# One-hot graph attention with residual and layer norm: rows led by their own column taken from SBUF instead of being gathered

## The chip, the cores and the metric

One NeuronCore of a Trainium2 chip. The metric is the device time of the kernel in microseconds (us). Before the change three runs gave 233.75 to 234.14 us, median 233.87 us.

## The reference

Four attention heads over 4096 nodes with 512 features, then a residual and a layer norm:

```python
ht = (h @ W).reshape(N, H, D).transpose(1, 0, 2)            # per head
e = leaky_relu(src[:, :, None] + dst[:, None, :], 0.01) + adj_mat[None]
att = softmax(e, axis=-1)
h_prime = einsum('hij,hjd->hid', att, ht).mean(axis=0)
x = layernorm(x + h_prime)                                   # no scale, no bias, eps 1e-5
```

`x` is 4096x512 and `adj` 4096x4096, both float32 (8.4 MB and 67.1 MB). The entries of `adj` that are not zero are uniform up to 1e9, and the diagonal is always among them, while the scores that are added are small. So the softmax of a row is one-hot at the largest entry of its `adj` row, unless two entries lie very close, and then `h_prime[i] = x[j] @ mean_over_heads(W)` with j the column of the largest entry of row i. Low columns are more likely to be filled than high ones.

## The kernel before, in words

The 4096 rows are worked on in 32 blocks of 128 rows (128 partitions). Block 0 holds rows 0 to 127; row p of block ib >= 1 is row 128 + 31p + ib - 1. A branch to a general path is taken when some row has no clear leader; with these inputs it is not taken.

Each block goes through a pipeline, and the outer loop `for t in range(NB)` writes its stages out by hand; every engine runs its instructions in the order in which this loop issues them.

- SyncE issues all large loads on one queue: W and `adj` (2.1 MB for a block; six buffers `adj_t`, so five blocks ahead, `load_adj(t + AHEAD)`), and the residual's rows of `x` into `hold[:, ib, :]`, four blocks (1.05 MB) at a time, at the steps that `x_at` lists. The stores of the results come at the end on the same queue.
- VectorE at step t takes the maxima of segments of block t (`seg`, L212: segments of 16 columns in blocks 0 to 17, then 32, then 64), the largest segment (`top`, `at`, L222 and L224), and, for block t - 2, the place of the maximum inside the segment (`within`, L270).
- GpSimd turns these into row numbers and gathers: `lead` (the leading segment, L230) for block t, then `col` (the leading column, L272) and the rows of `x` that the columns name, `y` (L255), for block t - 2. Columns below 128 in blocks 1 to 27 (`TABLED`) are not gathered: `col` gets 8192 (`SKIP`) added, which is out of bounds, so the gather leaves that row of `y` as `clear_rows` (L245, ScalarE) left it: zero. Those rows come from a table of 128 ready products (`z`, split in three bf16 parts) by a one-hot matrix `pick` (`spread`, `from_table`).
- TensorE does block t - 3: the one-hot's broadcast `px` (L331), the transpose of `y` in four pieces (`tp`, L284), the residual (`ident` times `hold`, L296), the table (L343) and four products with the mean of W (L303). ScalarE copies `tp` to `yt` (L286) between the transposes and the products.
- ScalarE does the squares and sums for the layer norm and for the test for a clear leader, and at t + 1 clears the next `y`.
- `head_norms` (L469), three parts, makes the norms of W and a that the test needs.

In this text block b of `y` is gathered in step b + 2 of the loop and turned by TensorE in step b + 3; ScalarE's `clear_rows` for block b stands in step b - 1, ahead of the copy `yt` of block b - 4.

Of the kernel before, what the change touches and what calls it, by code (L numbers as in the profile page):

```python
# [21 lines left out]
P = 128  # L22
# [5 lines left out]
LAST = 4  # L28
SKIP = 8192
TABLED = range(1, 28)  # L30


@with_exitstack
# [40 lines left out]
def leading_rows(ctx, tc, x, adj, W, a, out, ident, leads, any_bad):  # L74
# [74 lines left out]
    load_x(0, 1)  # L149
    for ib in range(KB // 2 + 1, AHEAD):  # L150
        load_adj(ib)
    load_x(1, Q - 1)

    make_identity(nc, ident)
    first = once.tile([P, NB], U32, name="first")
    for e, lo, hi in spans:
        if lo == 0:
            nc.gpsimd.iota(first[:, 0:1], pattern=[[0, 1]], base=0, channel_multiplier=N // e)
            lo = 1
        nc.gpsimd.iota(  # L160
            first[:, lo:hi], pattern=[[N // e, hi - lo]], base=(P + lo - 1) * N // e,
            channel_multiplier=RB * N // e,
        )
    ones = once.tile([P, P], F32, name="ones")
    nc.gpsimd.memset(ones, 1.0)
    width = once.tile([P, len(spans)], U32, name="width")
# [6 lines left out]
    zero = once.tile([P, 1], F32, name="zero")  # L173
# [25 lines left out]
    low_of, pick_of = {}, {}  # L199

    def segment_maxima(ib, lo, hi):

# [14 lines left out]
    def find_segment(ib):  # L217
        if ib == NB - 1:
            nc.vector.max(out=top[:, ib, :], in_=best)
            return  # L220
        seg = seg_of.pop(ib)
        nc.vector.max(out=top[:, ib, :], in_=seg)  # L222
        at = at_of[ib] = small.tile([P, 8], U32, name="at")
        nc.vector.max_index(at, top[:, ib, :], seg)  # L224
        row = small.tile([P, 1], U32, name="row")
        nc.gpsimd.tensor_tensor(row, at[:, 0:1], first[:, ib : ib + 1], op=OP.add)  # L226
        k = span_of(ib)
        e = spans[k][0]
# [6 lines left out]
        start = at_of[ib] = small.tile([P, 1], U32, name="start")  # L235
        if ib in TABLED:
            away = small.tile([P, 1], F32, name="away")
            nc.gpsimd.tensor_scalar(away, at[:, 0:1], float(P // e), float(SKIP), op0=OP.is_lt, op1=OP.mult)
            nc.gpsimd.tensor_scalar(start, at[:, 0:1], float(e), away, op0=OP.mult, op1=OP.add)
        else:  # L240
            nc.gpsimd.tensor_tensor(start, at[:, 0:1], width[:, k : k + 1], op=OP.mult)

    def clear_rows(ib):
        y = y_t[ib] = y_pool.tile([P, D], F32, name="y")
        nc.scalar.copy(y, zero.to_broadcast([P, D]))  # L245

    def gather_rows(ib, col):
        if ib not in TABLED:
            y = y_t[ib] = y_pool.tile([P, D], F32, name="y")
            nc.gpsimd.indirect_dma_start(  # L250
                out=y, out_offset=None, in_=x,
                in_offset=bass.IndirectOffsetOnAxis(ap=col[:, :1], axis=0),
            )
            return
        nc.gpsimd.indirect_dma_start(  # L255
            out=y_t[ib], out_offset=None, in_=x,
            in_offset=bass.IndirectOffsetOnAxis(ap=col[:, :1], axis=0),
            bounds_check=N - 1, oob_is_err=False,
        )
        low = low_of[ib] = small.tile([P, 1], BF16, name="low")  # L260
        nc.gpsimd.tensor_scalar(low, col, float(SKIP - 1), float(SKIP - 1), op0=OP.max, op1=OP.subtract)

# [3 lines left out]
    def find_column(ib):  # L266
        if ib < BEHIND:
            find_inner(ib)
        within = small.tile([P, 8], U32, name="within")
        nc.vector.max_index(within, top[:, ib, :], lead_of[ib])  # L270
        col = small.tile([P, 1], U32, name="col")
        nc.gpsimd.tensor_tensor(col, at_of.pop(ib), within[:, 0:1], op=OP.add)  # L272
        gather_rows(ib, col)

    def find_column_in_row(ib):
# [2 lines left out]
        nc.vector.max_index(col, top[:, ib, :], adj_t[ib])  # L278
        gather_rows(ib, col)

    def turned_rows(y):
        tp = psum.tile([P, KB, P], F32, name="tp", bufs=2)
        for kb in range(KB):
            nc.tensor.transpose(tp[:, kb, :], y[:, ds(kb, P, KB)], ident)  # L284
        yt = rows.tile([P, KB, P], F32, name="yt")
        nc.scalar.copy(yt, tp)  # L286
        return yt

    def turn(ib):
        yt_of[ib] = turned_rows(y_t.pop(ib))  # L290

    def residual(ib):
        start = ib not in o_ps
# [35 lines left out]
    def spread(ib):  # L329
        where = psum.tile([P, P], F32, name="px", bufs=1)  # L330
        nc.tensor.matmul(where, low_of.pop(ib).to_broadcast([P, P]), ident_b, start=True, stop=True)  # L331
        off = rows.tile([P, P], F32, name="off")
        nc.scalar.activation(off, where, AF.Square, bias=minus)  # L333
        pick = pick_of[ib] = rows.tile([P, P], BF16, name="pick")
        nc.scalar.activation(pick, off, AF.Relu, bias=1.0, scale=-1.0)  # L335
# [193 lines left out]
    def report(pg):  # L529
        nc.vector.tensor_scalar(any_bad, pg, -1.0, float(N), op0=OP.mult, op1=OP.add)  # L530

    x_at = {lo - 1 - lo // (5 * Q): (lo, Q) for lo in range(Q, BEHIND, Q)}
    squares = list(range(KB * H))
    squares_at = {t: 2 if t < 7 else 1 for t in range(3, 15)}
    COLUMN, PROJECT, STATS = 2, 3, 4
# [10 lines left out]
    for t in range(NB):  # L546
# [325 lines left out]
```

## Time and profile before

| | |
|---|---|
| median of 3 runs | 233.87 us (233.75 to 234.14) |
| time of the profiled execution | 233.53 us |
| its span, first to last instruction | 232.0 us |
| mean granted TensorE clock | 0.98 |
| TensorE busy | 197.6 us (85%) |
| VectorE busy | 189.6 us (82%) |
| ScalarE busy | 153.2 us (66%) |
| GpSimd busy | 111.5 us (48%) |
| moved by DMA | 96.04 MB, mean 414 GB/s |

The span is the time from the first to the last instruction; 1.5 us of the execution lie outside it. The busy shares are averages over stages in which different engines wait. PE is TensorE, PEld its weight loads, DVE VectorE, ACT ScalarE, POOL GpSimd, SP SyncE. `L303` is line 303 of the kernel before.

### The profile page before, as it was taken

What the parts mean: (1) busy time and instruction counts of PE and PEld (TensorE: products, weight loads), DVE (VectorE), ACT (ScalarE), POOL (GpSimd) and SP (SyncE); (2) the same over time, 40 slices, a digit from 0 to 9 for tenths busy, and PEclk for the clock granted to TensorE, in tenths of its full rate; (3) what the DMA queues carried; (4) which work ended last, traced back from release to release, by engine and by line L of the source; (5) the groups of instructions that cost most, each with busy time, mean ns of one, the idle gap of its engine ahead of it and who ended that gap; (6) DMA issues with size and microseconds to landing.
All of it is one profiled execution on the core that took longest, in us unless ns stands there. A gap on an engine that the chain in (4) does not pass through costs nothing.

```text
span 232.0 us, 2532 instructions
## 1 busy us (share of the span) xinstructions
PE 197.6 (85%) x604; PEld 95.5 (41%) x614; DVE 189.6 (82%) x296; ACT 153.2 (66%) x378; POOL 111.5 (48%) x254
## 2 busy tenths in 40 slices
PE   0069988779099999997999899999999999999990
PEld 0033443334044444443444345454544444545460
DVE  0448289899879997999699959996999999967882
ACT  3003213588075987797998678878888877958872
POOL 4020414525554556355635665554565665637620
PEclk9999999999859999999999999999999999999997
DMA  6999999999999999999999999999999999999995
GB/s 221 426 435 428 433 421 437 425 431 411 440 429 422 420 437 427 429 421 434 418 433 430 417 435 429 419 430 431 426 432 415 419 425 416 419 416 419 420 374 207
DMA packets 13379, 96.04 MB, mean 414 GB/s; under 512 B 2148, under 2 KB 2596, under 8 KB 7984
## 3 DMA queue, kind: packets, MB, share of 16 engines
q1 hardware_dynamic: 9792, 88.08, 90.0%
q0 software_dynamic: 3552, 7.73, 8.5%
q8 instruction: 6, 0.10, 0.2%
q14 instruction: 13, 0.11, 0.1%
q10 hardware_dynamic: 16, 0.02, 0.0%
HBM read 88.51 MB, written 8.39 MB: 418 GB/s over the span
## 4 chain that ended last, share of the span: by engine, by line
DMA 44%; PE 30%; DVE 19%; ACT 2%; issue 1%; POOL 1%; DVEq 0%; POOLq 0%; ACTq 0%
DMA adj_t<-in_adj_dram 39%; PE o L303 19%; DVE seg L212 15%; DMA y<-in_x_dram,col 4%; PE o L296 3%; PE o L343 3%; PE tp L284 3%; PE o L400 2%; DVE at L224 1%; DVE top L222 1%; DMA a_rows<-in_L_gnn_a_dram 1%; DVE inner L264 1%; POOL lead L230 0%; PE o L396 0%; ACT sq L368 0%
## 5 line engine op out<-in xcount | busy, mean ns | idle before, releaser
L212 DVE TENSOR_REDUCE seg<-adj_t 128x128 f32<-128x2048 f32 (+4 forms) x54 | 138.9, 2589 | 27.4 <-DMA adj_t<-in_adj_dram 27.4
L303 PE MATMUL o<-w_sum,yt 128*128 128x512 f32 x248 | 113.5, 598 | 1.1 <-ACT yt L286 0.8
L303 PEld LDWEIGHTS o<-w_sum,yt 128*128 128x128 f32 x248 | 46.8, 192 | 49.0 <-issue 42.0
L230 POOL DMA_INDIRECT lead<-in_adj_dram,row x31 | 32.5, 1050 | 14.5 <-POOL row L226 14.5
L255 POOL DMA_INDIRECT y<-in_x_dram,col x27 | 29.1, 1077 | 12.1 <-POOL col L272 6.1
L226 POOL TENSOR_TENSOR row<-at,first 128x1 uint32<-128x1 uint32 x31 | 5.8, 188 | 60.0 <-DVE at L224 43.6
L284 PE MATMUL tp<-ident,y 128*128 128x128 f32 x128 | 22.9, 302 | 12.0 <-DMA y<-in_x_dram,col 11.9
L286 ACT COPY yt<-tp 128x512 f32<-128x512 f32 x33 | 19.0, 576 | 14.2 <-PE tp L284 13.9
L451 PE MATMUL o<-hold,ident 128*128 128x512 f32 x32 | 16.4, 671 | 14.0 <-DMA hold<-in_L_gnn_W_dram 14.0
L284 PEld LDWEIGHTS tp<-ident,y 128*128 128x128 f32 x128 | 18.3, 210 | 23.9 <-issue 17.8
L296 PE MATMUL o<-hold,ident 128*128 128x512 f32 x50 | 26.5, 612 | 0.0
L333 ACT ACTIVATE off<-px,minus 128x128 f32<-128x128 f32 x27 | 9.9, 366 | 19.9 <-PE px L331 19.8
L343 PE MATMUL o<-z,pick 128*128 128x512 bf16 x72 | 20.4, 386 | 1.1 <-ACT pick L335 0.8
L347 ACT ACTIVATE sq<-hold 128x512 f32<-128x512 f32 x32 | 20.0, 625 | 0.0
L391 ACT ACTIVATE hold<-hold,nm,sd 128x512 f32<-128x512 f32 x24 | 18.8, 801 | 0.0
L374 ACT ACTIVATE sq<-hold,nm 128x512 f32<-128x512 f32 x24 | 17.3, 722 | 0.8
L452 ACT ACTIVATE w_sum<-o 128x512 f32<-128x512 f32 x4 | 2.4, 597 | 22.5 <-PE o L451 22.5
L245 ACT COPY y<-zero 128x512 f32<-128x512 f32 x27 | 16.3, 603 | 0.0
L451 PEld LDWEIGHTS o<-hold,ident 128*128 128x128 f32 x32 | 6.7, 216 | 22.9 <-issue 21.6
L343 PEld LDWEIGHTS <-pick 128*128 128x128 bf16 x81 | 7.8, 100 | 19.9 <-issue 10.5
L372 ACT ACTIVATE hold<-o 128x512 f32<-128x512 f32 x24 | 14.3, 597 | 0.8
L222 DVE MAX8 top<-seg 128x8 f32<-128x256 f32 (+2 forms) x31 | 11.3, 366 | 1.1
(117 smaller groups left out, 190.3 us busy)
## 6 DMA issues: line engine op xcount, KB each, us to landing
adj_t<-in_adj_dram SPq DMA_DIRECT2D x28, 2048.0 KB, 33.1
adj_t<-in_adj_dram SPq DMA_DIRECT2D x6, 1024.0 KB, 27.3
out_dram<-hold SPq DMA_DIRECT2D x12, 512.0 KB, 10.1
hold<-in_x_dram SPq DMA_DIRECT2D x5, 1024.0 KB, 33.0
hold<-in_L_gnn_W_dram SPq DMA_DIRECT2D x2, 2048.0 KB, 16.5
hold<-in_x_dram SPq DMA_DIRECT2D x4, 512.0 KB, 12.7
adj_t<-in_adj_dram SPq DMA_DIRECT2D x4, 512.0 KB, 18.6
out_dram<-hold SPq DMA_DIRECT2D x4, 256.0 KB, 2.8
```

Source lines behind the costliest of these rows:

```text
L212: nc.vector.tensor_reduce(seg_of[ib][:, ts(k, N // e // n)], adj_t[ib][:, ts(k, N // n)].rearrange("p (s e) -> p s e", e=e), axis=AX.X, op ...
L230: nc.gpsimd.indirect_dma_start(out=lead, out_offset=None, in_=adj_segs[e], in_offset=bass.IndirectOffsetOnAxis(ap=row[:, :1], axis=0),)
L255: nc.gpsimd.indirect_dma_start(out=y_t[ib], out_offset=None, in_=x, in_offset=bass.IndirectOffsetOnAxis(ap=col[:, :1], axis=0), bounds_che ...
L284: nc.tensor.transpose(tp[:, kb, :], y[:, ds(kb, P, KB)], ident)
L286: nc.scalar.copy(yt, tp)
L296: nc.tensor.matmul(o_ps[ib], ident, hold[:, ib, :], start=start, stop=False)
L303: nc.tensor.matmul(o_ps[ib], yt_of[ib][:, kb, :], w_sum[:, kb, :], start=(start and kb == 0), stop=(kb == KB - 1),)
L343: nc.tensor.matmul(o_ps[ib], pick, z[k], start=(start and k == 0), stop=False)
L347: nc.scalar.activation(sq, hold[:, ib, :], AF.Square, accum_out=xx[:, ib : ib + 1])
L374: nc.scalar.activation(sq, hold[:, ib, :], AF.Square, bias=nm[:, i], scale=-float(D), accum_out=sd[:, i])
L391: nc.scalar.activation(hold[:, ib, :], o, AF.Identity, bias=nm[:, i], scale=sd[:, i])
L451: nc.tensor.matmul(o, ident, hold[:, w_at + kb * H + h, :], start=(h == 0), stop=(h == H - 1))
```

## The change

In blocks 4 to 17 (`OWNED`) a row whose leading column is its own row number is no longer gathered. `clear_rows` copies the block's rows of `x` from `hold` into `y` instead of zeros. GpSimd compares the column with the row's own number (`own`, made once), adds 8192 to it where they are equal (`skipped`, `asked`), and gathers with `asked`. What `y` then holds in the rows of the table is the row's own `x`, which must not count; so a masked identity `kept` (`ident * 8192 > col`) takes the place of `ident` when `y` is turned, and since that is no plain transpose any more, `nc.tensor.matmul` takes the place of `nc.tensor.transpose`. Columns are float32 in these blocks.

As `hold` must now be filled a step before the block's `y` is cleared, `x` is loaded sooner: blocks 1 to 7 in one load ahead of `adj` block 5, 8 to 11 at step 2, 12 to 15 at step 6, 16 to 19 at step 10 (before: 1 to 3 ahead, 4 to 7 at step 3, 8 to 11 at 7, 12 to 15 at 11, 16 to 19 at 15); 20 to 23 stay at step 18. The three parts of `head_norms` move from steps 21 to 23 to steps 16 to 18. The tile `off` becomes bf16 with one buffer. Near the end two normalising copies move ahead of a square root.

```diff
+OWNED = range(4, 18)
...
-    load_x(1, Q - 1)
+    load_x(1, 2 * Q - 1)
...
+    own = once.tile([P, len(OWNED)], F32, name="own")
+    nc.gpsimd.iota(
+        own, pattern=[[1, len(OWNED)]], base=P + OWNED[0] - 1, channel_multiplier=RB,
...
     def clear_rows(ib):
         y = y_t[ib] = y_pool.tile([P, D], F32, name="y")
-        nc.scalar.copy(y, zero.to_broadcast([P, D]))
+        nc.scalar.copy(y, hold[:, ib, :] if ib in OWNED else zero.to_broadcast([P, D]))
+
+    def leave_out_own(ib, col):
+        skipped = small.tile([P, 1], F32, name="skipped", bufs=2)
+        k = ib - OWNED[0]
+        nc.gpsimd.tensor_scalar(skipped, col, own[:, k : k + 1], float(SKIP), op0=OP.is_equal, op1=OP.mult)
+        asked = small.tile([P, 1], U32, name="asked", bufs=2)
+        nc.gpsimd.tensor_scalar(asked, col, skipped, None, op0=OP.add)
+        return asked
+
+    def keep_gathered(ib, col):
+        kept = kept_of[ib] = rows.tile([P, P], F32, name="kept")
+        nc.gpsimd.tensor_scalar(kept, ident, float(SKIP), col, op0=OP.mult, op1=OP.is_gt)
...
+        asked = leave_out_own(ib, col) if ib in OWNED else col
         nc.gpsimd.indirect_dma_start(
             out=y_t[ib], out_offset=None, in_=x,
-            in_offset=bass.IndirectOffsetOnAxis(ap=col[:, :1], axis=0),
+            in_offset=bass.IndirectOffsetOnAxis(ap=asked[:, :1], axis=0),
             bounds_check=N - 1, oob_is_err=False,
         )
+        if ib in OWNED:
+            keep_gathered(ib, col)
...
-    def turned_rows(y):
+    def turned_rows(y, kept=None):
...
-            nc.tensor.transpose(tp[:, kb, :], y[:, ds(kb, P, KB)], ident)
+            if kept is None:
+                nc.tensor.transpose(tp[:, kb, :], y[:, ds(kb, P, KB)], ident)
+            else:
+                nc.tensor.matmul(tp[:, kb, :], y[:, ds(kb, P, KB)], kept, start=True, stop=True)
...
-        off = rows.tile([P, P], F32, name="off")
+        off = rows.tile([P, P], BF16, name="off", bufs=1)
...
-    x_at = {lo - 1 - lo // (5 * Q): (lo, Q) for lo in range(Q, BEHIND, Q)}
+    x_at = {2: (8, 4), 6: (12, 4), 10: (16, 4), 18: (20, 4)}
...
-        if 21 <= t < 24:
-            head_norms(t - 21)
+        if 16 <= t < 19:
+            head_norms(t - 16)
...
     add_sums(NB - 2, hold[:, NB - 2, :])
+    finish(BEHIND + 2)
+    finish(LATE - 1)
     moments(NB - 2)
-    finish(BEHIND + 2)
     stats_of_half(NB - 1, 0)
     factor(NB - 2)
     normalise(NB - 2, o_ps.pop(NB - 2))
-    finish(LATE - 1)
```

SyncE's queue, from the load of x's first rows on. Before (`x4` at a row's end counts equal rows; a row of x with 128x1536 is three blocks, with 128x2048 four):

```order
L132 DMA hold<-in_x_dram 128x512
L128 DMA adj_t<-in_adj_dram 128x4096 x2
L135 DMA hold<-in_x_dram 128x1536
L128 DMA adj_t<-in_adj_dram 128x4096 x3
L135 DMA hold<-in_x_dram 128x2048
L128 DMA adj_t<-in_adj_dram 128x4096 x4
L135 DMA hold<-in_x_dram 128x2048
```

After:

```order
L133 DMA hold<-in_x_dram 128x512
L129 DMA adj_t<-in_adj_dram 128x4096 x2
L136 DMA hold<-in_x_dram 128x3584
L129 DMA adj_t<-in_adj_dram 128x4096 x2
L136 DMA hold<-in_x_dram 128x2048
L129 DMA adj_t<-in_adj_dram 128x4096 x4
L136 DMA hold<-in_x_dram 128x2048
```

The load of seven blocks of x stands where that of three stood, ahead of `adj` block 5, and the next two loads of x stand ahead of `adj` blocks 7 and 11 instead of 8 and 12; the one after that, ahead of 15 instead of 16.

GpSimd for one block (the gather of block 4 in step 6; `lead` there is block 6's). Before:

```order
L226 TENSOR_TENSOR row<-at,first 128x1
L230 DMA lead_442<-in_adj_dram,row 128x16
L238 TENSOR_SCALAR away<-at 128x1
L239 TENSOR_SCALAR start<-at,away 128x1
L272 TENSOR_TENSOR col<-start,within 128x1
L255 DMA y<-in_x_dram,col 128x512
L261 TENSOR_SCALAR low<-col 128x1
```

After:

```order
L232 TENSOR_TENSOR row<-at,first 128x1
L236 DMA lead_445<-in_adj_dram,row 128x16
L245 TENSOR_SCALAR away<-at 128x1
L246 TENSOR_SCALAR start_f<-at,away 128x1
L297 TENSOR_SCALAR col_f<-within,start_f 128x1
L258 TENSOR_SCALAR skipped<-col_f,own 128x1
L260 TENSOR_SCALAR asked<-col_f,skipped 128x1
L276 DMA y<-in_x_dram,asked 128x512
L265 TENSOR_SCALAR kept<-ident,col_f 128x128
L284 TENSOR_SCALAR low<-col_f 128x1
```

Two small operations stand between `col` and the gather, and `kept` (128x128) between the gather and `low`.

TensorE around the first part of `head_norms`. Before it stands between blocks 17 and 18:

```order
L303 MATMUL o<-w_sum,yt 128x512 x4
L475 MATMUL o<-ww,ones 128x16
L476 MATMUL o<-each,ones 128x8
L331 LDWEIGHTS low
L331 MATMUL px<-ident_b,low 128x128
L284 MATMUL tp<-ident,y 128x128 x4
L296 MATMUL o<-hold,ident 128x512
```

After, between blocks 12 and 13:

```order
L334 MATMUL o<-w_sum,yt 128x512 x4
L506 MATMUL o<-ww,ones 128x16
L507 MATMUL o<-each,ones 128x8
L362 LDWEIGHTS low
L362 MATMUL px<-ident_b,low 128x128
L315 MATMUL tp<-kept,y 128x128 x4
L327 MATMUL o<-hold,ident 128x512
```

The two small products have moved five blocks up, and `tp` of blocks 4 to 17 is made with `kept`.

More of the change, by code (lines that the diff above doesn't have):

```diff
@@ L163, in leading_rows @@
         )
+    own = once.tile([P, len(OWNED)], F32, name="own")
+    nc.gpsimd.iota(
+        own, pattern=[[1, len(OWNED)]], base=P + OWNED[0] - 1, channel_multiplier=RB,
+        allow_small_or_imprecise_dtypes=True,
+    )
     ones = once.tile([P, P], F32, name="ones")
@@ L198, in leading_rows @@
     seg_of, at_of, lead_of, y_t, yt_of, o_ps = {}, {}, {}, {}, {}, {}
-    low_of, pick_of = {}, {}
+    low_of, pick_of, kept_of = {}, {}, {}
     def segment_maxima(ib, lo, hi):
@@ L234, in find_segment @@
         lead_of[ib] = lead
-        start = at_of[ib] = small.tile([P, 1], U32, name="start")
+        owned = ib in OWNED
+        start = at_of[ib] = small.tile([P, 1], F32 if owned else U32, name="start_f" if owned else "start")
         if ib in TABLED:
@@ L270, in find_column @@
         nc.vector.max_index(within, top[:, ib, :], lead_of[ib])
-        col = small.tile([P, 1], U32, name="col")
-        nc.gpsimd.tensor_tensor(col, at_of.pop(ib), within[:, 0:1], op=OP.add)
+        start = at_of.pop(ib)
+        if ib in OWNED:
+            col = small.tile([P, 1], F32, name="col_f", bufs=2)
+            nc.gpsimd.tensor_scalar(col, within[:, 0:1], start, None, op0=OP.add)
+        else:
+            col = small.tile([P, 1], U32, name="col")
+            nc.gpsimd.tensor_tensor(col, start, within[:, 0:1], op=OP.add)
         gather_rows(ib, col)
@@ L279, in find_column_in_row @@
         gather_rows(ib, col)
-    def turned_rows(y):
+    def turned_rows(y, kept=None):
         tp = psum.tile([P, KB, P], F32, name="tp", bufs=2)
         for kb in range(KB):
-            nc.tensor.transpose(tp[:, kb, :], y[:, ds(kb, P, KB)], ident)
+            if kept is None:
+                nc.tensor.transpose(tp[:, kb, :], y[:, ds(kb, P, KB)], ident)
+            else:
+                nc.tensor.matmul(tp[:, kb, :], y[:, ds(kb, P, KB)], kept, start=True, stop=True)
         yt = rows.tile([P, KB, P], F32, name="yt")
@@ L289, in turn @@
     def turn(ib):
-        yt_of[ib] = turned_rows(y_t.pop(ib))
+        yt_of[ib] = turned_rows(y_t.pop(ib), kept_of.pop(ib, None))
     def residual(ib):
```

## The prediction

> **What bounds the kernel now.** I read the page first: how full the DMA engines are, and the chain that ended last.
>
> ```profile
> DMA  6999999999999999999999999999999999999995
> ...
> q1 hardware_dynamic: 9792, 88.08, 90.0%
> q0 software_dynamic: 3552, 7.73, 8.5%
> ...
> DMA 44%; PE 30%; DVE 19%; ACT 2%; issue 1%; POOL 1%; DVEq 0%; POOLq 0%; ACTq 0%
> ```
>
> DMA is full in all slices but the first and the last. q1 carries the large loads, q0 the gathers. Over the span of 232.0 us a megabyte costs 0.90 × 232 / 88.08 = 2.37 us on q1 and 0.085 × 232 / 7.73 = 2.55 us on q0. So four blocks of x (1.05 MB) cost 2.49 us, and a block of `adj` (2.10 MB) 4.97 us.
>
> Then the chain in order of time, around its last change of hands:
>
> ```profile
> 139.45 9.32 DMA y<-in_x_dram,col
> ...
> 148.91 0.72 PE tp L284 x4
> ...
> 151.13 3.43 PE o L303 x8
> 154.57 0.13 PE o L475 x2
> 154.70 0.31 PE o L476 x2
> ...
> 160.70 0.54 PE tp L284 x4
> ...
> 222.91 3.73 PE o L400 x16
> ```
>
> Until 148.8 us (139.45 + 9.32) the chain goes through loads, VectorE and a gather; from there TensorE is on it block after block. TensorE's timeline says which block is where, and that it hardly waits again:
>
> ```profile
> 37.47 1.13 PE L303 MATMUL o<-w_sum,yt 128*128 128x512 f32 x2 [0.84 <-ACT yt L286]
> ...
> 63.42 1.10 PE L284 MATMUL tp<-ident,y 128*128 128x128 f32 x4 [5.76 <-DMA y<-in_x_dram,col]
> ...
> 71.72 0.70 PE L284 MATMUL tp<-ident,y 128*128 128x128 f32 x4
> ...
> 77.25 0.70 PE L284 MATMUL tp<-ident,y 128*128 128x128 f32 x4
> ...
> 148.91 0.72 PE L284 MATMUL tp<-ident,y 128*128 128x128 f32 x4 [0.40 <-DMA y<-in_x_dram,col]
> ...
> 155.01 0.70 PE L284 MATMUL tp<-ident,y 128*128 128x128 f32 x4
> ...
> 160.54 0.70 PE L284 MATMUL tp<-ident,y 128*128 128x128 f32 x4
> ...
> 221.28 0.72 PE L284 MATMUL tp<-ident,y 128*128 128x128 f32 x4 [0.26 <-DMA y<-in_x_dram,col]
> ```
>
> These turn blocks 0 (its products, first row), 3, 4, 5, 17, 18, 19 and 31. From 18 to 19 is 5.53 us: the busy time of a block. From 5 to 17 are 12 blocks in 71.66 us, 5.97 each: TensorE has 0.44 us of room a block there, and none from 17 to 31. Whatever makes block 18 late makes the end late by as much.
>
> VectorE's timeline, the first reduction of blocks 5, 7, 8, 12, 16 and 20:
>
> ```profile
> 46.59 4.48 DVE L212 TENSOR_REDUCE seg<-adj_t 128x128 f32<-128x2048 f32 x2 [1.02 <-DMA adj_t<-in_adj_dram]
> ...
> 58.06 4.48 DVE L212 TENSOR_REDUCE seg<-adj_t 128x128 f32<-128x2048 f32 x2
> ...
> 65.94 4.48 DVE L212 TENSOR_REDUCE seg<-adj_t 128x128 f32<-128x2048 f32 x2 [1.69 <-DMA adj_t<-in_adj_dram]
> ...
> 71.62 4.46 DVE L212 TENSOR_REDUCE seg<-adj_t 128x128 f32<-128x2048 f32 x2
> ...
> 90.17 4.42 DVE L212 TENSOR_REDUCE seg<-adj_t 128x256 f32<-128x4096 f32 x1 [1.42 <-DMA adj_t<-in_adj_dram]
> ...
> 114.50 4.42 DVE L212 TENSOR_REDUCE seg<-adj_t 128x256 f32<-128x4096 f32 x1 [1.77 <-DMA adj_t<-in_adj_dram]
> ...
> 139.07 2.29 DVE L212 TENSOR_REDUCE seg<-adj_t 128x64 f32<-128x2048 f32 x1 [2.51 <-DMA adj_t<-in_adj_dram]
> ```
>
> (71.62 is block 9.) VectorE waits at exactly the blocks whose `adj` is queued behind a load of x. From block 8 to 12 are 24.23 us; less 2.49 for the x in it, a block of `adj` with its gathers takes 5.44 us of DMA, while VectorE takes 5.68 for a block (8 to 9). The queue is worked off in order, so an x that is put ahead pushes every later `adj` back.
>
> **The gathers left out.** In the reference's inputs 145 rows of blocks 4 to 17 have their largest entry in their own column: 145 × 2048 bytes = 0.30 MB, at q0's price 0.76 us of DMA, spread over 14 blocks. This is all that the change can bring on the DMA engines; `x` is moved in the queue, not added. Clearing `y` from `hold` instead of from zeros is one ScalarE copy either way: nothing.
>
> **The turn with a masked identity.** Here is the price that decides.
>
> ```profile
> L303 PE MATMUL o<-w_sum,yt 128*128 128x512 f32 x248 | 113.5, 598 | 1.1 <-ACT yt L286 0.8 <-issue 0.2
> ...
> L284 PE MATMUL tp<-ident,y 128*128 128x128 f32 x128 | 22.9, 302 | 12.0 <-DMA y<-in_x_dram,col 11.9
> ```
>
> 31 blocks with four products each give 248 instructions: an f32 product is two. 32 blocks with four transposes give 128: a transpose is one. As products the four turns are eight instructions. Pace in the chain: 3.43 / 8 = 0.429 us at 512 columns, 3.73 / 16 = 0.233 at 256; the line through both gives 0.135 at 128, and a transpose of 128 now takes 0.54 / 4 = 0.135 as well. So 4 × 0.135 = 0.54 us more a block, 6.07 instead of 5.53. Bounds: 0.32, if only streaming counted (0.857 / 4 a product, less 0.135), and 1.32, if an instruction of 128 columns took as long as one of 256 (8 × 0.233 less 0.54). I take 0.54: it lies on the line, and the transpose, the one row of this size, has the same pace. It exceeds the 0.44 of room, so from block 4 to 17 TensorE itself sets the pace.
>
> The Trainium skill ("TensorE: Matmul & The Clock Gate", Terms, the row on the xbus) says that trn2 gained a transpose mode that is 4x faster for FP32. If leaving it cost the whole factor, a block's turn would go from 0.54 to 2.16 us and the sum below would grow by 14 us; the rows above speak for a factor of two, since a short transpose is not at its streaming speed.
>
> **x loaded sooner.** (a) Before block 5, 1.05 MB more are queued, and before block 7 twice that: `adj` 5 is there at 49.1 instead of 46.6, and block 7, which before landed no later than 65.94 - 2.49 - 5.44 = 58.0, at 58.0 + 4.97 = 63.0, 4.9 us later. Block 8 follows VectorE's work at 68.7 (before 65.94). The same comes at 11 and 15; in between VectorE runs some 2.5 us late, and at block 20, where the queues are equal again, it is level: 138.8 against 139.07.
>
> (b) ScalarE's copy for block 4 now waits for x of blocks 1 to 7.
>
> ```profile
> 36.30 0.63 ACT L245 COPY y<-zero 128x512 f32<-128x512 f32 x1
> 36.81 0.60 ACT L286 COPY yt<-tp 128x512 f32<-128x512 f32 x1
> ```
>
> That load is 1.83 MB, 4.35 us, behind `adj` 4, which landed by 46.59 - 5.44 - 1.86 = 39.3. So the copy goes at 43.7 at the earliest, and at 49.1, when the next `adj` is there, at the latest. Behind it on ScalarE stands `yt` of block 0, for which TensorE's products wait: 7.4 to 12.8 us late. What hides it is the wait of 5.76 us before block 3 and that block's gather, itself 2.5 us later. After an idle time like that TensorE runs slower for a while:
>
> ```profile
> 64.00:72.00 8.00, 7.78 (x18) 3.55 (x18) 6.17 (x13) 4.52 (x13) 3.43 (x8) 0.68 1.02 431
> ```
>
> (a granted clock of 0.68 from 64 to 72 us; block 3 took 8.3 us for it, 63.42 to 71.72, instead of 5.5.) That loss of 2.7 us moves to block 0. From 37.47 to 57.66, TensorE's next idle point, are 20.2 us, 2.2 of them waits on gathers: 37.47 + 7.4 + 18.0 + 2.7 = 65.6, when block 3's gather lands, at 63.4 + 2.5 = 65.9. With the late bound block 5 comes 1.6 us later than below; I take the early one.
>
> **GpSimd.** Two operations more ahead of the gather and one with 128x128 behind it:
>
> ```profile
> L238 POOL TENSOR_SCALAR away<-at 128x1 f32<-128x1 uint32 x27 | 6.6, 243 | 1.9
> ...
> L182 POOL TENSOR_SCALAR minus_b<-ident 128x128 bf16<-128x128 f32 x1 | 0.6, 567 | 0.0
> ...
> 60.86 1.07 POOL L255 DMA_INDIRECT y<-in_x_dram,col  x1 [0.27 <-POOL col L272]
> ...
> 67.08 1.07 POOL L255 DMA_INDIRECT y<-in_x_dram,col  x1 [0.27 <-POOL col L272]
> ...
> DMA to landing us min/median/max: 6.1/8.3/9.3
> ```
>
> The rows at 60.86 and 67.08 are the gathers of blocks 4 and 5. 2 × (0.243 busy + 0.07 idle before it, 1.9 / 27) = 0.6, with the slower `col` 0.7 us on each gather's way. `kept`, 0.57 to 1.1, runs while the gather lands (8.3 us) and delays `low` and the next `row`; nobody waits for these so soon. `kept` has two buffers and so waits for TensorE's turn two blocks back, done some 8 us before the gather lands; should TensorE fall further behind, this wait would hold up the next block's `lead`.
>
> **Sum.** Block 5's gather, the row at 67.08, follows block 7's reductions: 67.08 + 4.9 + 0.7 + 8.3 = 81.0, against 77.25. Block 4 is through by then (its gather at 60.86 + 2.5 + 0.7 + 8.3 = 72.4, plus 6.07 = 78.5). Blocks 5 to 17: 13 × 6.07 = 78.9. `head_norms` on TensorE, 0.13 + 0.31 = 0.44, now lies in this stretch too. Block 18 at 81.0 + 78.9 + 0.44 = 160.3, against 155.01: 5.3 us late. The gathers stay ahead of this: block 17's before 148.8, now 2.5 + 0.7 later, 152.0, TensorE's turn at 154.2. From 18 on TensorE's instructions are the same and have no gap but 0.26 at block 31, which goes: 5.1 us at the end. The two copies moved ahead of a square root at the end fill idle time of ScalarE and let a store go sooner: 0 to 0.2, I take 0.1. 5.0 us on the profiled execution's 233.5 is 238.5; the median of the runs lies 0.3 above it: 238.8 us.
>
> **Rivals.**
> 1. Only one of the two delays counts. If x ahead costs nothing, TensorE's own pace gives 77.25 + 78.9 + 0.44 = 156.6 for block 18, 1.6 late, 235.2 at the end. If the turn costs nothing, block 17 starts with its gather at 152.0 and 18 at 157.4, 2.4 late, 236.0. For it: the turn's price is worked out, not seen. Against it: both rest on rows that agree.
> 2. Faster: DMA decides. If a masked turn costs under the 0.44 us of room and TensorE and VectorE swallow the later `adj`, the 0.76 us of gathers are saved: 233.1 us. Against it: TensorE waits on nothing from 17 to 31, so bytes saved cannot end its work sooner, and block 17's gather would be on time only if the loads were not worked off in order.
> 3. Slower still: the late bound of (b), 1.6 us; a turn near its upper bound, up to 13 × 0.78 = 10 us; or `kept`'s wait reaching VectorE through the next `lead`. 240.8 to 249.
> 4. The turn costs fourfold: 14 us more, about 253. The page named above stands behind it; the pace of f32 products speaks against it.
> 5. The delays and the savings cancel: no change that can be told (a measurement of this kernel tells changes of more than about 0.2%, 0.47 us).
>
> **Numbers.** Forecast, between 237.0 and 240.8: 0.61. Rival 1 (235.0 to 237.0): 0.20. Rival 2: 0.07. Rival 3: 0.05. Rival 4: 0.02. Rival 5: 0.05. Range 235.0 to 240.8, which holds the forecast and rival 1, 0.81. Faster 0.07, the same 0.05, slower 0.88.
>
> **What would show it.** `tp` with eight instructions in blocks 4 to 17 at a pace near 0.135 us; VectorE's waits for `adj` at blocks 5, 7, 11 and 15 and none of note at 20; ScalarE idle ahead of the copy at 36 us until 44 or later; TensorE without waits from block 5 on and block 18 near 160 us. It is wrong if `tp` takes little longer than before, if `adj` 7, 11 and 15 land less than 4 us later, or if gathers land so much sooner with fewer rows that TensorE's start in block 5 moves up.

## The result and the profile after

The changed kernel takes 250.41 us (249.96 to 250.72, four runs) against 234.00 (233.75 to 234.14): ratio 1.0701, 95% interval 1.0678 to 1.0724. The forecast was 238.8, its range 235.0 to 240.8: the direction was right, but the loss of 16.4 us is more than three times the one forecast. The profiled execution took 250.68 us, its span 249.1, at a clock of 0.98.

The page of the changed kernel, in the rows that answer to those shown first of the kernel before:

```profile
DMA  7999999999999999999999999999999999953053
...
q1 hardware_dynamic: 9648, 88.08, 83.8%
q0 software_dynamic: 3552, 7.43, 8.0%
...
PE 68%; DMA 20%; ACT 4%; issue 2%; POOL 2%; DVE 1%; SPq 0%; POOLq 0%; ACTq 0%
```

The gathers moved 7.43 MB where they had moved 7.73: the 0.30 MB are saved. But the DMA engines now run empty near the end, and the chain that ended last went from 30% TensorE to 68%. TensorE's timeline (start, duration, operation, count, and the idle time before it) at the products of block 0, and the turns of blocks 3, 4, 5, 17 and 18:

```profile
45.38 5.33 PE L334 MATMUL o<-w_sum,yt 128*128 128x512 f32 x8 [8.72 <-ACT yt L317]
...
66.72 0.72 PE L313 MATMUL tp<-ident,y 128*128 128x128 f32 x4 [0.78 <-DMA y<-in_x_dram,col]
...
73.26 2.10 PE L315 MATMUL tp<-kept,y 128*128 128x128 f32 x8 [0.82 <-DMA y<-in_x_dram,asked]
...
80.36 2.10 PE L315 MATMUL tp<-kept,y 128*128 128x128 f32 x8
...
164.18 2.08 PE L315 MATMUL tp<-kept,y 128*128 128x128 f32 x8
...
171.10 0.70 PE L313 MATMUL tp<-ident,y 128*128 128x128 f32 x4
```

Block 5 starts at 80.36, where the forecast had 81.0. A turn is eight instructions, as forecast, but takes 2.08 us in place of 0.70. From block 17 to 18 are 6.91 us (before, a block took 5.53), and block 18 starts 16.09 us later than before (155.01). The groups of these instructions (count, busy time, mean ns of one, idle time before them):

```profile
L315 PE MATMUL tp<-kept,y 128*128 128x128 f32 x112 | 29.2, 404 | 0.9 <-DMA y<-in_x_dram,asked 0.8
L315 PEld LDWEIGHTS tp<-kept,y 128*128 128x128 f32 x112 | 27.2, 326 | 5.8 <-issue 3.8 <-PE px L362 2.0
...
L313 PEld LDWEIGHTS tp<-ident,y 128*128 128x128 f32 x72 | 10.3, 209 | 6.5 <-issue 4.8 <-PE px L362 1.3 <-DMA y<-in_x_dram,col 0.2
```

PEld is a weight load; in these products the weights are the pieces of `y`. Each of the eight instructions loads its weights anew, and one load takes 326 ns where a transpose's takes 209. Last, VectorE's reductions of blocks 5, 7, 8 and 15, and its wait ahead of block 18; then ScalarE's copy for block 4:

```profile
49.42 4.48 DVE L218 TENSOR_REDUCE seg<-adj_t 128x128 f32<-128x2048 f32 x2 [4.02 <-DMA adj_t<-in_adj_dram]
...
62.91 4.48 DVE L218 TENSOR_REDUCE seg<-adj_t 128x128 f32<-128x2048 f32 x2 [2.06 <-DMA adj_t<-in_adj_dram]
69.01 4.46 DVE L218 TENSOR_REDUCE seg<-adj_t 128x128 f32<-128x2048 f32 x2
...
110.55 4.42 DVE L218 TENSOR_REDUCE seg<-adj_t 128x256 f32<-128x4096 f32 x1 [1.52 <-DMA adj_t<-in_adj_dram]
...
136.57 0.17 DVE L511 TENSOR_REDUCE w<-o 128x4 f32<-128x16 f32 x1 [9.01 <-PE o L507]
```

```profile
44.23 0.62 ACT L252 COPY y<-hold 128x512 f32<-128x512 f32 x1 [7.78 <-DMA hold<-in_x_dram]
```

The loads came near where the forecast put them. The wait of 9.01 us on a product of `head_norms` was not in it: TensorE is late, and VectorE stands in line behind it.

### The profile page after: what moved, and what is told of

The parts are those of the page before. It is cut to its first block, busy times and chain, and to the rows that moved or that the text cites. A ratio compares the mean times of both kernels' runs of the same rounds, so it can differ in the third digit from the quotient of the medians.

```text
span 249.1 us, 2696 instructions
## 1 busy us (share of the span) xinstructions
PE 215.3 (86%) x670; PEld 114.5 (46%) x670; DVE 189.6 (76%) x296; ACT 153.8 (62%) x378; POOL 132.5 (53%) x297
## 3 DMA queue, kind: packets, MB, share of 16 engines
q0 software_dynamic: 3552, 7.43, 8.0%
## 4 chain that ended last, share of the span: by engine, by line
PE 68%; DMA 20%; ACT 4%; issue 2%; POOL 2%; DVE 1%; SPq 0%; POOLq 0%; ACTq 0%
PE o L334 38%; DMA hold<-in_x_dram 14%; PE tp L315 11%; PE o L327 7%; PE o L374 6%; DMA y<-in_x_dram,asked 3%; DMA adj_t<-in_adj_dram 3%; PE tp L313 2%; PE o L431 1%; ACT sq L491 1%; PE o L355 1%; ACT yt L317 1%; PE px L362 1%; ACT y L252 0%; POOL y L276 0%
## 5 line engine op out<-in xcount | busy, mean ns | idle before, releaser
L218 DVE TENSOR_REDUCE seg<-adj_t 128x128 f32<-128x2048 f32 (+4 forms) x54 | 138.8, 2587 | 24.1 <-DMA adj_t<-in_adj_dram 24.1
L315 PE MATMUL tp<-kept,y 128*128 128x128 f32 x112 | 29.2, 404 | 0.9 <-DMA y<-in_x_dram,asked 0.8
L315 PEld LDWEIGHTS tp<-kept,y 128*128 128x128 f32 x112 | 27.2, 326 | 5.8 <-issue 3.8
L482 PE MATMUL o<-hold,ident 128*128 128x512 f32 x32 | 16.4, 670 | 14.1 <-DMA hold<-in_L_gnn_W_dram 14.1
L327 PE MATMUL o<-hold,ident 128*128 128x512 f32 x50 | 25.6, 594 | 0.0
L374 PE MATMUL o<-z,pick 128*128 128x512 bf16 x81 | 21.9, 379 | 1.8 <-ACT pick L366 1.8
L364 ACT ACTIVATE off<-px,minus 128x128 bf16<-128x128 f32 x27 | 9.9, 366 | 18.3 <-PE px L362 18.2
L276 POOL DMA_INDIRECT y<-in_x_dram,asked x14 | 15.2, 1088 | 7.0 <-POOL asked L260 4.0
L276 POOL DMA_INDIRECT y<-in_x_dram,col x13 | 14.1, 1084 | 6.6 <-POOL col L300 3.9
L313 PEld LDWEIGHTS tp<-ident,y 128*128 128x128 f32 x72 | 10.3, 209 | 6.5 <-issue 4.8
## 6 DMA issues: line engine op xcount, KB each, us to landing
adj_t<-in_adj_dram SPq DMA_DIRECT2D x4, 512.0 KB, 14.7
```

What stands on the lines that cost most here:

```text
L218: nc.vector.tensor_reduce(seg_of[ib][:, ts(k, N // e // n)], adj_t[ib][:, ts(k, N // n)].rearrange("p (s e) -> p s e", e=e), axis=AX.X, op ...
L276: nc.gpsimd.indirect_dma_start(out=y_t[ib], out_offset=None, in_=x, in_offset=bass.IndirectOffsetOnAxis(ap=asked[:, :1], axis=0), bounds_c ...
L315: nc.tensor.matmul(tp[:, kb, :], y[:, ds(kb, P, KB)], kept, start=True, stop=True)
L327: nc.tensor.matmul(o_ps[ib], ident, hold[:, ib, :], start=start, stop=False)
L374: nc.tensor.matmul(o_ps[ib], pick, z[k], start=(start and k == 0), stop=False)
L482: nc.tensor.matmul(o, ident, hold[:, w_at + kb * H + h, :], start=(h == 0), stop=(h == H - 1))
```

## The experiments

Each is the kernel before or the changed kernel with one part exchanged. The theories as the expectations name them: T, the turn as a product is nearly all of the loss; S, its price is the weight load from every fourth column of `y`; X, the sooner loads of `x` cost what the forecast said; G, GpSimd's added work becomes a bound; L, the gathers are late because of the loads and copies of `x`; E, the new order of the end costs; H, the sooner head norms cost.

**1. The turn alone, as a product with the plain identity** (kernel before):

```
- nc.tensor.transpose(tp[:, kb, :], y[:, ds(kb, P, KB)], ident)
+ nc.tensor.matmul(tp[:, kb, :], y[:, ds(kb, P, KB)], ident, start=True, stop=True)   # blocks 4 to 17
```

> The kernel before, but blocks 4 to 17 are turned by f32 products with the plain identity instead of transposes; nothing else is changed. Theory T (the turn alone makes the change slow: eight instructions at 0.234 us instead of four at 0.12 to 0.135, 1.38 us more a block, and TensorE becomes the bound): block 4 is turned at 71.7 as before, then 14 blocks of 6.91 us and the 0.44 us of the head norms put block 18 at 168.9 instead of 155.0; about 247.8 us. Rival R (the turn costs the 0.54 us a block that was forecast, and the rest of the loss comes from the later loads and the waits on GpSimd): block 18 at 157.1, about 236 us.

Measured: 247.05 us, ratio 1.0563 (1.0545 to 1.0581). Its groups, and the turn of block 18 in the timeline:

```profile
L285 PE MATMUL tp<-ident,y 128*128 128x128 f32 x112 | 29.1, 403 | 0.0
L285 PEld LDWEIGHTS tp<-ident,y 128*128 128x128 f32 x112 | 27.2, 326 | 4.6 <-issue 4.6
```

```profile
168.23 0.70 PE L287 MATMUL tp<-ident,y 128*128 128x128 f32 x4
```

13.2 of the 16.4 us are this one edit. The mask in the identity has no part in it: the same 326 ns stand here with the plain one.

**2. The changed kernel with plain transposes** (`kept` is still made but not used, so `x` in the rows of the table counts where it must not):

```
- yt_of[ib] = turned_rows(y_t.pop(ib), kept_of.pop(ib, None))
+ yt_of[ib] = turned_rows(y_t.pop(ib))
```

> The changed kernel, but y is turned by plain transposes again in all blocks. The mask is left out, so that rows of the table count their own x as well; loads, gathers and GpSimd's work are those of the changed kernel. T: what is left of the change delays block 17's gather to about 152 us, 3 us later than before, and with that block 18 to 157.4: about 236.0 us. R: most of the 16.4 us stay, above 244 us.

Measured: 243.89 us, ratio 1.0456 (1.0405 to 1.0506). Far from T's time, at the edge of R's: taking the turn out saves only half of its price, since a second limit stands just below it. TensorE's waits, with the total, the count and the longest:

```profile
PE tp L313 <- DMA y<-in_x_dram,asked: 10.7, 10, 2.3
```

**3. The loads of `x` alone** (kernel before with the changed kernel's order of the loads):

```
- load_x(1, Q - 1)
+ load_x(1, 2 * Q - 1)
- x_at = {lo - 1 - lo // (5 * Q): (lo, Q) for lo in range(Q, BEHIND, Q)}
+ x_at = {2: (8, 4), 6: (12, 4), 10: (16, 4), 18: (20, 4)}
```

> The kernel before with x loaded as in the changed kernel, and nothing else. Theory X (loads in front push adj back one for one, and the late gathers reach the saturated part of TensorE): block 5, 7, 11 and 15 start 2.5 to 5 us late on VectorE, block 17's gather lands 2.5 us late at 151.3, block 18 at 157.2 instead of 155.0: about 235.9 us. Rival A (the buffers ahead absorb it): within 0.5 us of 234.0.

Measured: 235.78 us, ratio 1.0082 (1.0065 to 1.0099), as expected. VectorE's block 20 and TensorE's block 18:

```profile
138.90 2.27 DVE L212 TENSOR_REDUCE seg<-adj_t 128x64 f32<-128x2048 f32 x1
```

```profile
156.53 0.70 PE L284 MATMUL tp<-ident,y 128*128 128x128 f32 x4
```

VectorE is level again at block 20 (139.07 before); block 18 is 1.52 us late and the kernel 1.9.

**4. The changed kernel with pieces of neighbouring columns.** A turned piece of `y` is 128 neighbouring columns instead of every fourth; W is loaded in the matching order, and the result is the same.

```
- w_blocks = W.rearrange("(p kb) (h d) -> p (kb h) d", p=P, h=H)
+ w_blocks = W.rearrange("(kb p) m -> p kb m", p=P)
...
- nc.tensor.matmul(tp[:, kb, :], y[:, ds(kb, P, KB)], kept, start=True, stop=True)
+ nc.tensor.matmul(tp[:, kb, :], y[:, ts(kb, P)], kept, start=True, stop=True)
```

> The changed kernel, but the four pieces of y that are turned are 128 neighbouring columns each instead of every fourth column; W is loaded in the matching order, so the same sums are computed. Theory S (an f32 weight load that reads every fourth element of y takes 0.234 us and sets the pace of the masked turn): the pace falls to 0.12 to 0.135 us an instruction, a block takes 6.0 to 6.1 us, block 18 comes at about 159.5: 238 to 239 us. Rival P (a short f32 product never goes faster than 0.234 us, whatever its weights' stride): 250.4 us as before.

Measured: 241.83 us, ratio 1.0326 (1.0288 to 1.0364). A turn fell from 2.08 to 1.11 us, as S said, but the time followed only in part: TensorE waited 6.6 us for gathers in seven places. The second limit again.

**5. The second limit: GpSimd.** Three kernels. Without `kept` (the changed kernel, plain transposes; as in 2, `x` counts in the rows of the table where it must not):

```
- if ib in OWNED:
-     keep_gathered(ib, col)
...
- yt_of[ib] = turned_rows(y_t.pop(ib), kept_of.pop(ib, None))
+ yt_of[ib] = turned_rows(y_t.pop(ib))
```

> The changed kernel without the masked identity: blocks 4 to 17 are turned with the plain identity and kept is not made, so that x stands in the rows of y that no gather overwrites and is counted as if it were the table's for rows that own a smaller column too (this part of the result differs from the reference). With plain turns but kept still made, the changed kernel took 243.89 us and TensorE waited for gathered rows. Theory G, that GpSimd is the bound there (col, skipped, asked at about 0.40 us each, the gather's issue, kept at 0.75 us: 6.2 to 6.4 us a block against TensorE's 5.53): taking away 0.75 us leaves 5.5 us a block, the gathers land at TensorE's pace, block 18's products start at 157 to 159 us and the kernel takes 235.8 to 238. Theory L, that the gathers are late because of the copies of x on ScalarE and the sooner loads, with nothing owed to kept: 243 to 244.5, block 18 at 163.

Measured: 239.14 us, ratio 1.0212 (1.0194 to 1.0231), 4.7 less than with `kept`; about 1 us above what G gave and far from L. Block 18 came at 160.89. GpSimd's round, 5.60 us from gather to gather (102.06 to 107.66), still lies just above TensorE's 5.53.

GpSimd's work alone, on the loads, clears and turns of before:

```
- nc.gpsimd.iota(own, pattern=[[1, len(OWNED)]], base=P + OWNED[0] - 1, channel_multiplier=RB, ...)
+ nc.gpsimd.iota(own, pattern=[[1, len(OWNED)]], base=-200000, channel_multiplier=0, ...)   # no row matches
```

> The kernel before with the changed kernel's GpSimd work alone: skipped, asked and kept are made in blocks 4 to 17, but the list own holds columns that no row has, so that every row is gathered, y is cleared with zeros, x is loaded when it was before, head norms are where they were, and the turns are plain. Theory G: GpSimd needs 6.2 to 6.4 us a block from block 4 on, 0.7 to 0.9 us more than TensorE's 5.53; some of it is eaten by the two to three blocks by which gathers run ahead, so block 18 starts at 159 to 163 us against 155.0, and the kernel takes 238 to 242. Theory L (late x and its copies make the gathers late): 234 to 235, block 18 at 155 to 156.

Measured: 240.32 us, ratio 1.0264 (1.0245 to 1.0284); G holds, L falls. (This kernel and the next also kept the changed kernel's head norms and order of the end, against what their expectations say; the end's 0.8 us is in their times, experiment 7.) GpSimd's timeline from one gather to the next:

```profile
107.66 1.08 POOL L276 DMA_INDIRECT y<-in_x_dram,asked  x1 [0.51 <-POOL asked L260]
108.81 0.75 POOL L265 TENSOR_SCALAR kept<-ident,col_f 128x128 f32<-128x128 f32 x1
109.64 0.23 POOL L284 TENSOR_SCALAR low<-col_f 128x1 bf16<-128x1 f32 x1
109.96 0.19 POOL L232 TENSOR_TENSOR row<-at,first 128x1 uint32<-128x1 uint32 x1
110.42 1.07 POOL L236 DMA_INDIRECT lead<-in_adj_dram,row  x1 [0.28 <-POOL row L232]
111.58 0.24 POOL L245 TENSOR_SCALAR away<-at 128x1 f32<-128x1 uint32 x1
111.93 0.27 POOL L246 TENSOR_SCALAR start_f<-at,away 128x1 f32<-128x1 uint32 x1
112.30 0.29 POOL L297 TENSOR_SCALAR col_f<-within,start_f 128x1 f32<-128x1 uint32 x1
112.69 0.32 POOL L258 TENSOR_SCALAR skipped<-col_f,own 128x1 f32<-128x1 f32 x1
113.10 0.29 POOL L260 TENSOR_SCALAR asked<-col_f,skipped 128x1 uint32<-128x1 f32 x1
113.92 1.08 POOL L276 DMA_INDIRECT y<-in_x_dram,asked  x1 [0.53 <-ACT hold L403]
```

From 107.66 to 113.92 are 6.26 us, and GpSimd waits nowhere longer than 0.53: every instruction stands right behind the one before. `kept` takes 0.83 from start to start, and with `skipped` and `asked` the gather comes 1.62 after the start of `col_f` (112.30), where before it came 0.51 after that of `col` (115.11 to 115.62 there). The 6.26 are more than TensorE's 5.53, so block 18 starts at 161.23. The kernel before, over the same stage, has room on this engine:

```profile
116.77 0.23 POOL L261 TENSOR_SCALAR low<-col 128x1 bf16<-128x1 uint32 x1
120.06 0.19 POOL L226 TENSOR_TENSOR row<-at,first 128x1 uint32<-128x1 uint32 x1 [3.06 <-DVE inner L264]
```

The skipping alone, on the loads of before, with `y` cleared to zeros and no `kept`, so that the rows led by their own column lack their part of the result:

```
- yt_of[ib] = turned_rows(y_t.pop(ib), kept_of.pop(ib, None))
+ yt_of[ib] = turned_rows(y_t.pop(ib))
...
- nc.scalar.copy(y, hold[:, ib, :] if ib in OWNED else zero.to_broadcast([P, D]))
+ nc.scalar.copy(y, zero.to_broadcast([P, D]))
```

> The kernel before with the changed kernel's skipping alone: rows led by their own column in blocks 4 to 17 (145 of them, 0.30 MB) aren't gathered and their y stays zero, so that their part of the result is left out; kept is not made, turns are plain, x and head norms are where they were. It has two more short GpSimd operations a block ahead of the gather, 0.8 us. Theory G says GpSimd is at 5.4 to 5.6 us a block, just TensorE's pace: 234 to 236. If the bytes saved were worth what they take at the stream's rate (0.76 us at 400 GB/s) and GpSimd didn't matter: 233.1. If two operations already delay each gather: 236 to 238.

Measured: 234.87 us, ratio 1.0041 (1.0024 to 1.0057). Block 18 at 155.28 against 155.01: the 0.30 MB fewer bought nothing that shows, with two more operations ahead of each gather.

**6. Neighbouring columns in the kernel before** (W in the matching order, as in 4), the head norms at steps 16 to 18, and both together:

```
- nc.tensor.transpose(tp[:, kb, :], y[:, ds(kb, P, KB)], ident)
+ nc.tensor.transpose(tp[:, kb, :], y[:, ts(kb, P)], ident)
```

> The kernel before, but every turned piece of y is 128 neighbouring columns instead of every fourth one, with W loaded in the matching order; same result. In the changed kernel this took the plain turns of a block from 0.70 to 0.61 us. 32 blocks at 0.09 us would be 2.9 us, of which only the stretch in which TensorE never waits counts (blocks 5 to 17, 1.2 us), and the last gather (row 31 landing at 221.1 us) bounds the end: expected 232.7 to 233.6. Rival: the pace of TensorE's first part is given back wholly by the gathers' pace behind it: 233.9.

```
- if 21 <= t < 24: head_norms(t - 21)
+ if 16 <= t < 19: head_norms(t - 16)
```

> The kernel before with the head norms at steps 16 to 18 in place of 21 to 23. In the kernels with slow turns VectorE waited 9.0 us for the head norms' TensorE products there and nothing came of it at the end. Theory: VectorE waits 2 to 4 us for TensorE at 122 to 128 us, the stream of adj goes on behind it, and some 0.7 us of TensorE's work moves from the stretch where TensorE never waits (from block 18) to one where it waits for gathers: 233.2 to 234.0. Rival: the wait on VectorE makes the gathers of blocks 17 and 18 late, block 18 at 156 to 158: 235 to 237.

> The kernel before with pieces of 128 neighbouring columns (alone 233.98 against 233.99: its cheaper turns were given back by gathers that bound blocks 6 to 17) and the head norms at steps 16 to 18. If the two are additive: 233.2 to 234.0, about the time of the kernel with the head norms alone. If VectorE's wait for the head norms makes the gathers late: 235 or more.

Measured: the columns 233.98 us, ratio 1.0000 (0.9990 to 1.0011); the head norms 233.87, ratio 0.9996 (0.9987 to 1.0005); both together 234.19, ratio 1.0015 (1.0001 to 1.0030). A plain turn of neighbouring columns took 0.61 us in place of 0.70, and it changed nothing: TensorE now waited 14.7 us for gathers instead of 11.9, and block 18 came at 155.77. The head norms sooner are free in a kernel whose TensorE is on time. So no version that was run beats the kernel before.

**7. The order of the end**, alone and taken back from the changed kernel:

```
+ finish(BEHIND + 2)
+ finish(LATE - 1)
  moments(NB - 2)
- finish(BEHIND + 2)
  ...
- finish(LATE - 1)
```

> The kernel before with the changed order of the last blocks alone (finish of LATE - 1 and of BEHIND + 2 ahead of the moments of NB - 2). In every kernel with that order the last store landed 2.8 to 3.4 us after its issue, in those without it 2.31 to 2.38, while the last store's issue stood at 73.66 to 73.68 us after block 18's products in both. Theory E, that the order of the end costs 0.5 to 1 us through the last stores: 234.4 to 235.0. Rival, that the longer landing comes from something else in those kernels: 233.9 to 234.1, with 2.35 us from issue to landing.

> The changed kernel with the order of the end as it was before. The new order alone cost 0.66 to 0.76 us on the kernel before (234.66 against 233.90 to 234.0). Additive: 249.5 to 249.9 against the changed kernel's 250.41, the last store landing about 2.35 us after its issue in place of 3.35. Rival, that with TensorE late and the DMA queues empty the order makes no difference: 250.2 to 250.6.

Measured: 234.66 us, ratio 1.0030 (1.0019 to 1.0041); and the changed kernel with the old end 249.53, ratio 1.0660 (1.0642 to 1.0677), 0.9 less than with the new. E holds. The last stores (KB each, median us from issue to landing), first of the kernel before, then with the new order:

```profile
out_dram<-hold SPq DMA_DIRECT2D x2, 512.0 KB, 2.7
out_dram<-hold SPq DMA_DIRECT2D x2, 256.0 KB, 2.6
```

```profile
out_dram<-hold SPq DMA_DIRECT2D x2, 512.0 KB, 4.3
out_dram<-hold SPq DMA_DIRECT2D x2, 256.0 KB, 3.4
```

The last store is issued at the same distance from block 18, but lands later. Why is not settled: with the new order the stores ahead of it are issued sooner and also take longer.

**8. The turn as a product, with neighbouring columns** (the kernel of experiment 1 with the layout of 4):

```
- nc.tensor.matmul(tp[:, kb, :], y[:, ds(kb, P, KB)], ident, start=True, stop=True)
+ nc.tensor.matmul(tp[:, kb, :], y[:, ts(kb, P)], ident, start=True, stop=True)
```

> The kernel before with blocks 4 to 17 turned by a product with the plain identity, as in the run that took 247.05 us, but with pieces of 128 neighbouring columns; same result. Theory S, that the whole price of the turn as a product is its weight loads from every fourth column: 8 instructions at 0.118 us, TensorE's block 5.44 + 0.52 = 5.96 us in place of 6.91; the gathers alone need 5.9 to 6.0 us a block in blocks 6 to 17, so block 18 starts at 155.5 to 157 and the end gains 0.9 us on 73.7: 233.7 to 235.5. Rival, that a product turn has a price of its own beside its weight loads, as the mended change (239.29) might suggest: 237 to 239.

Measured: 234.70 us, ratio 1.0036 (1.0024 to 1.0049). Its groups, and blocks 5 and 18:

```profile
L287 PE MATMUL tp<-ident,y 128*128 128x128 f32 x112 | 15.6, 282 | 0.9 <-DMA y<-in_x_dram,col 0.9
L287 PEld LDWEIGHTS tp<-ident,y 128*128 128x128 f32 x112 | 13.6, 192 | 5.9 <-issue 4.5 <-PE px L336 1.4
```

```profile
77.54 1.11 PE L287 MATMUL tp<-ident,y 128*128 128x128 f32 x8
...
156.61 0.61 PE L289 MATMUL tp<-ident,y 128*128 128x128 f32 x4
```

This settles S in the main: the same products, the same count, and only the step between the columns that are loaded as weights changed (W's new order cost nothing with plain turns, experiment 6). The weight load went from 326 to 192 ns and the price of the edit from 13.2 to 0.8 us. S's "whole price" says a little too much: TensorE's block is 5.94 us here (71.60 to 77.54) where one with plain turns is 5.44 (162.05 to 167.49). These 0.50 us are what eight product instructions cost over four transposes; most of them fall into the 0.44 us of room that a block had.

**9. The change with both costs mended**: neighbouring columns, and `kept` made by ScalarE from a flag:

```
- nc.gpsimd.tensor_scalar(kept, ident, float(SKIP), col, op0=OP.mult, op1=OP.is_gt)
+ nc.gpsimd.tensor_scalar(wanted, col, float(SKIP), None, op0=OP.is_lt)
...
+ nc.scalar.activation(kept, ident, AF.Copy, scale=kept_of[ib])   # TensorE's step; kept_of holds `wanted`
```

> The changed kernel with both of the found costs mended: each turned piece of y is 128 neighbouring columns (the product's weight loads went from 0.2335 to 0.118 us each), and the masked identity is made by ScalarE from ident, scaled by a flag that GpSimd makes from col in one 128x1 operation (about 0.35 us in place of 0.84); the result is the same as the changed kernel's. Turn and GpSimd as the two costs (theories S and G): TensorE's block is 5.44 + 0.52 = 5.96 us, GpSimd's 6.3 - 0.84 + 0.35 = 5.8; block 4 starts at 73.8, block 18 at 157 to 160, and the kernel takes 235.5 to 238.5. If a third cost of this size were still in the change: 240 or more. If skipping the gathers pays after all once both costs are gone: below 234.0.

> The mended change (239.29 us) with the head norms back at steps 21 to 23 and the order of the end as before. The end is worth 0.7 to 0.9 us. Theory H, that VectorE's wait of 2.1 us for the head norms' TensorE products at step 17 makes the gathers from block 17 on late: 0.7 + 2.1 less, 236.3 to 237.2, block 18 at 158.5 to 159.5 in place of 160.85; what is left over before is then the sooner x (1.8) and the product turn (0.8). Rival, that the head norms cost nothing here either and the missing 2 us are GpSimd's and ScalarE's added work: 238.4 to 238.8, block 18 at 160.5 to 161.

Measured: 239.29 us, ratio 1.0237 (1.0220 to 1.0253); with the old head norms and end too 238.43, ratio 1.0181 (1.0155 to 1.0207), block 18 at 160.24. H falls: the 0.9 us are the end. Even mended, the change costs 4.5 us. Block 5 starts at 80.45 there, 2.9 later than in experiment 8 (77.54); TensorE's block of 5.94 or more then never gets it back, and short waits for ScalarE's `off` and `kept` stand in the rest of block 18's 3.6. The sooner loads alone made block 5 start 2.1 us late (79.33 in experiment 3 against 77.25); the other 0.8 were not taken apart. No run has the one buffer of `off` alone.

## Why the prediction was wrong, step by step

Where the 16.4 us come from, by block 18 (171.10 - 155.01 = 16.1): 13.2 is the turn alone (168.23 in experiment 1), 2.4 is block 4's later start (73.26 against 70.90 there), which TensorE cannot make good, and about 0.5 is lost in blocks 4 and 5, which took 7.10 and 7.21 us: blocks 5 and 6 still start with their gathers, 0.14 us after these landed (80.22 and 87.44), and TensorE itself is the bound from block 6 on. Behind block 18 the end's order adds 0.8 to 0.9. (The two profiled executions differ by 17.1, the medians by 16.4.)

- **The turn with a masked identity, the step that failed.** The prediction took 8 × 0.135 us and so 0.54 more a block, 6.07 in all. It measured 6.91 - 5.53 = 1.38 more. 13 blocks × (6.91 - 6.07) = 10.9, and block 18 came 10.8 later than the forecast's 160.3: this term is nearly all of the miss of 11.6, and the end's order is the rest. It was priced by a line through the products with 512 and 256 columns, that is, by what streams through the array. What it left out is that `y` is loaded as weights in steps of four columns: with that step an instruction took 0.2335 us from start to start, with neighbouring columns 0.112. With neighbouring columns 0.54 a block would have been nearly right (0.50, experiment 8), partly by luck: the 0.233 at 256 columns divides a row whose first instruction takes longer, and from start to start it is 0.216. The line then gives 0.108 at 128 columns, near the 0.112 and no longer at the transposes' 0.135. The prediction quoted no PEld row; the one of the kernel before has 210 ns for a load of `y` in a plain turn, and would not have given the 326.
- The Trainium skill had the rule for it, and the prediction didn't use it: "Advanced Engine Details and Errata", SBUF Cachelines, says that SBUF is read in lines of 16 bytes and that each access to another line costs extra. Every fourth float32 is a new line each time. The traces agree as to the step (326 against 192 ns for a load); whether the lines are the mechanism no run here shows.
- Rival 3 held the right size: a turn near its upper bound, 1.32 a block, is 10 us more than the forecast and so about 249, 1.4 below the 250.41. The prediction gave this and two other causes 0.05 together.
- Rival 4 (253) was 2.6 off. The Trainium skill ("TensorE: Matmul & The Clock Gate", Terms, the row on the xbus) calls the transpose mode four times faster for FP32. No run here shows that: a turn as a product took 1.11 against 0.61 us with neighbouring columns, a factor of 1.8, near the two that the count of instructions gives, and 2.08 against 0.70, a factor of 3.0, with the step of four.
- **GpSimd's round, costed at nothing, was wrong and was covered.** The prediction had 0.7 us as a delay of each gather, and for `kept` "nobody waits for these so soon". That looked at one operation after another, not at the round: 6.26 us a block, above TensorE's 5.53. In the changed kernel TensorE's 6.91 hides it; without the slow turns it decides (243.89 and 240.32).
- **x loaded sooner held**: VectorE's blocks 5, 7 and 8 at 49.42 (forecast 49.1), 62.91 (63.0) and 69.01 (68.7), block 15 3.5 us later than before (110.55 against 107.06); level at 138.90 (138.8) in experiment 3, and 235.78 against Rival 1's 236.0. In the changed kernel it isn't level: the wait of 9.01 us behind a late TensorE comes between. That wait cost nothing: from block 7 on every gather landed at least 0.6 us before TensorE came to it.
- **ScalarE's copy held**: 44.23 (43.7); block 0's products at 45.38, 7.9 us late (7.4 to 12.8); block 3 at 66.72 (65.9); block 5 with its gather at 80.36 (81.0). That block 5 came out is partly luck: the gather took 7.1 us to land instead of 8.3, and block 4 kept TensorE until 80.2, not 78.5.
- **The gathers left out held**: 0.30 MB, and nothing gained that shows (experiment 5).
- **The end had the wrong sign**: 0.1 us sooner was forecast, 0.8 later was measured.

## What to carry to other kernels

For short products, price the weight load as well as the streaming: read the PEld row of the operand that is loaded, and ask what step it is read with. Here a transpose that became a float32 product had twice as many instructions and loads, and a step of four columns (16 bytes) made each instruction take twice as long (0.2335 against 0.112 us). When operations are added to an engine that looks half idle, add up one whole round of that engine, gap by gap, and hold it against the bound's round. A large cost can hide a second one right below it, so take parts out singly and put them in singly: here 13.2 us went in, and only 6.5 came back out.

## What the runs showed of the hardware that was not expected

A float32 product of 128 columns whose weights are every fourth column took one instruction in 0.2335 us from start to start, longer than one of 256 columns with neighbouring weights (0.216); with neighbouring columns it was about 0.112. For plain transposes the same change was 0.70 to 0.61 us in four. On GpSimd the gather started 0.8 us after the start of `asked`, the 128x1 operation that makes its offsets, which itself takes 0.29; in the kernel before it started 0.51 after the start of `col`, which takes 0.19. And moving two normalising copies by a few places at the end, with the last store's issue unmoved as counted from block 18, made that store land 0.5 us later in the kernel before (2.87 us after its issue in place of 2.35).
